# The row of q scores: spread over all partitions by two DMAs instead of eight TensorE transposes

## The chip, the cores and the metric

The kernel runs on one core of a Trainium2 chip, in one launch. The metric is device time in microseconds (us). Five engines work side by side, each through its own list of instructions in order: TensorE (PE in the profile; its weight loads are PEld), VectorE (DVE), ScalarE (ACT), GpSimd (POOL) and SyncE (SP, which here only issues DMAs). Between two instructions of different engines, and between a DMA and its reader, stands a semaphore wait.

## The reference

Two layers on x of 32 batches, each batch C x N = 512 x 1024 in float32; adj is 512 x 512. Cut to what matters:

```python
# layer 0, per batch
q = einsum('c,cn->n', wq, x)                  # 1024 scores
k = einsum('c,cn->n', wk, x)                  # 1024 scores
scores = q[None, :] + k[:, None]              # [m, n]
scores = where(scores > 0, scores, 0.01 * scores)
att = softmax(scores, axis=-1)
agg = einsum('cn,mn->cm', x, att)
x = layernorm(x + relu(adj @ agg + bm))
# layer 1
x = layernorm(x + einsum("nf,nm->mf", x, adj * adj) + bias)
```

In layer 1 `W = adj * adj` elementwise (support and kernel are both adj), and `out[m] = sum_n x[n] W[n, m] + bias`.

## The kernel before

The softmax over a sum q + k with one kink needs no 1024 x 1024 matrix. For each column m the scores above zero are those whose q is over -k, so the kernel sorts: it finds each q's rank, scatters the rows of (adj x)^T to DRAM in the order of q, forms running sums upwards and downwards along the sorted rows, writes both as a table to DRAM, and gathers for every m the one row of the table at which its k falls. Two running sums, weighted and divided, are the softmax-weighted mix.

One batch passes through these steps (short names as they stand in the order lists):

- `ld` loads x (four DMAs of 512 KB, SP). `pa` (PE) computes q and k of the batch in four column groups of 256 (rows 0, 32, 64 and 96 of a PSUM tile hold q, the rows after them k). `pc` (ACT) copies that to SBUF as `part`, 128 x 256. `co` (PE) turns `part` and `cc` (DVE) picks from it `s.qk`: q and k as columns, one element per partition and tile.
- `ro` and `rc` make the **row**: q along the free dimension, the same 1024 values on every partition. `ro` (line 247) is eight TensorE transposes of a column of `s.qk` broadcast to 128 x 128, into a 4 KB PSUM tile; `rc` (line 256) is one DVE instruction that copies the PSUM tile to SBUF as `qb` and takes its maximum on the way (line 261), and two small ones. `qb` has one buffer.
- `rk` (DVE, line 267, eight per batch) compares `qb` with a column of q and counts: ranks. `ct` (ACT, line 281, eight per batch) does it with k by a Sign activation. Both write a `junk` tile that nobody reads.
- `z` (PE, eight of 1/8 batch) is adj x; `zc` (ACT) copies it to `zt`, which has one buffer; `sc` (POOL) scatters it by rank. `sl` loads the sorted rows, `se` (ACT) makes the exponentials, `u` and `d` (DVE) the running sums inside a partition, `cu`, `cd` (PE) and `uc`, `dc` (ACT) the carries over partitions, `tu`, `td`, `te` (DVE) add them, `tw`, `tl` (SP) write the table.
- `g` (POOL) gathers, `mw`, `ms`, `mx` mix, `t` (PE) turns the mix back, `r` (DVE) adds the residual, `s0`, `rt`, `rce`, `n0` (ACT, DVE) are the first layernorm.
- Layer 1 is one level of a Strassen-Winograd product: `t1` to `t4` (DVE) form the sums of quarters of x, `U 11 Z V Y 12 21` (PE) are the seven products (with the bias added by a small bf16 matmul whose stationary operand is `first_0` or `first_10`, 6 x 128), `Uc Vc Zc up lr ll ls` collect them, `s1 r1 n` normalize and `st` stores (four DMAs of 512 KB per batch, SP).

Nothing but order decides when an instruction is issued. `emit` walks three lists of words such as `ro.-1` or `rk.-1.7` (step, batch relative to the iteration, part): `head`, then `loop` once for each of b = 12 to 25, then `tail`. Each word appends its instructions to its engine's list, so the order of words that share an engine is that engine's order. In one iteration of `loop`, layer 1 of batch b-4, the mix of b-3, the table of b-2, the ranks of b-1 and the scores of b are under way. In the list before, `ro.-1` stands near the start of the iteration, followed by `rc.-1` and the ranks; the last part of a batch's `z` (`z.-2.7`) falls into the next iteration:

```
    td.-3.1 ro.-1 tw.-3.0 n0.-4.3 z.-2.7 n0.-4.0 tw.-3.1 tl.-3 t1.-4 rc.-1 U.-4.0 rk.-1.7 U.-4.1
```

A tile of a pool with a tag takes the next buffer of that tag, and its first writer waits until everything that used the buffer before is done. The tags touched here are `qb` (1 buffer), `part`, `carry`, `T2` and `junk_s` (1 each), and `w`: two PSUM tiles of 4 KB, shared by the q row, the four turns and the two `pair` products of a batch.

Of the kernel before, what the change touches and what calls it, by code (L numbers as in the profile page):

```python
# [42 lines left out]
P = 128  # L43
# [6 lines left out]
def adj_resnorm_kernel(  # L50
# [48 lines left out]
    nbm = const.tile([P, CT], F32, name="nbm")  # L99
# [21 lines left out]
    eps = const.tile([P, 1], F32, name="eps")  # L121
    nc.vector.memset(eps, EPS)
    power = const.tile([P, CT], F32, name="power")
# [12 lines left out]
    zero = one.tile([P, ZR], F32, tag="carry", name="zero")[0:1, :]  # L136
    nc.vector.memset(zero, 0.0)
    sorted_z = [dr.tile([N, ZR], F32, name=f"sorted_z_{i}") for i in range(2)]
# [3 lines left out]
    spare = const.tile([1, 1], F32, name="spare")  # L142
# [7 lines left out]
    first_0 = const.tile([6, P], BF16, name="first_0")  # L150
    first_10 = const.tile([6, P], BF16, name="first_10")
# [25 lines left out]
    def bias_parts(b):  # L177


        own = const.tile([6, 8], F32, name="own")  # L180
# [4 lines left out]
        nc.vector.tensor_copy(first_0, own[:, 4:5].broadcast_to([6, P]))  # L185
        nc.vector.memset(first_10, 1.0)
        rest, done = room[:, 0, :], room[:, 1, :]
        for i in range(3):
            part = one.tile([P, N], BF16, tag="junk_s", name=f"bias_part_{i}")[0:6, 0:H]
            nc.vector.tensor_copy(part, rest)  # L190
            if i < 2:
                nc.vector.tensor_tensor(rest, rest, part, ALU.subtract)
            if i == 0:
                nc.vector.tensor_scalar(done, part, own[:, 0:1], None, ALU.mult)
            else:
                nc.vector.scalar_tensor_tensor(
                    done, part, own[:, i : i + 1], done, ALU.mult, ALU.add
                )
# [27 lines left out]
    def parts_copy(b):  # L226
        s = st[b]
        s.part = one.tile([P, Q], F32, tag="part", name=f"part_{b}")
        nc.scalar.copy(s.part, s.ps)
# [8 lines left out]
    def cols_copy(b):  # L238
        s = st[b]
        s.qk = s4.tile([P, NT, 2], F32, tag="qk", name=f"qkc_{b}")  # L240
# [5 lines left out]

    def row(b):

        s = st[b]
        s.ps = p2.tile([P, N], F32, tag="w", name=f"q_tp_{b}")  # L250
        for j in range(NT):
            nc.tensor.transpose(
                s.ps[:, j * P : (j + 1) * P], s.qk[:, j, 0:1].broadcast_to([P, P]), ident
            )

    def row_copy(b):
        s = st[b]
        s.qb = one.tile([P, N], F32, tag="qb", name=f"qb_{b}")
        top = s4.tile([P, 3], F32, tag="top", name=f"top_{b}")
        s.top, s.ntop = top[:, 0:1], top[:, 1:3]  # L260
        nc.vector.tensor_scalar(s.qb, s.ps, 1.0, None, ALU.mult, ALU.max, accum_out=s.top)  # L261
# [19 lines left out]
    def count(b, j):  # L281
        s = st[b]
        junk = one.tile([P, N], BF16, tag="junk_s", name=f"junk_s_{b}_{j}")
        nc.scalar.activation(  # L284
            junk, s.qb, AF.Sign, bias=s.k[:, j : j + 1], accum_out=s.sign[:, j : j + 1]
        )
# [111 lines left out]
    def carry_down_copy(b):  # L398
        st[b].carry = one.tile([P, ZR], F32, tag="carry", name=f"carry_{b}")
# [62 lines left out]
    def stats(b, name):  # L462
        return [sp.tile([P, CT], F32, tag=t + name, name=f"{t}{name}_{b}") for t in ("tot", "var")]

    def spread(b, i, t, v, name):

        junk = one.tile([P, N], BF16, tag="junk_s", name=f"junk_{name}_{b}_{i}")
# [30 lines left out]
    def root0(b):  # L498
            v = st[b].v0
            nc.scalar.activation(v[1], v[1], AF.Sqrt, scale=1.0 / N**3, bias=eps)  # L500

    def root0_end(b):
            v = st[b].v0
            nc.vector.reciprocal(v[1], v[1])  # L504
    
# [39 lines left out]
    def rows1(b, m):  # L545
        s = st[b]
        if not s.v1:
            s.v1 = stats(b, "1")
            s.nb = sp.tile([P, CT], F32, tag="nb", name=f"nb_{b}")
            s.part2 = sp.tile([P, CT], F32, tag="part2", name=f"part2_{b}")  # L550
# [84 lines left out]
    def store(b, m):  # L635
# [7 lines left out]
        "rc": row_copy, "rk": rank, "re": rank_end, "ct": count, "ce": count_end,  # L643
# [21 lines left out]
    bias.0 ld.1 ld.2 ld.3 pa.0 z.0.0 pc.0 co.0 zc.0.0 z.0.1 cc.0 ro.0 zc.0.1 pa.1 rc.0 ct.0.1  # L665
    rk.0.1 z.0.2 ct.0.3 rk.0.7 pc.1 rk.0.2 ct.0.5 z.0.4 rk.0.3 ct.0.2 rk.0.4 ct.0.7 rk.0.6 z.0.6
    zc.0.4 zc.0.2 rk.0.0 rk.0.5 co.1 zc.0.6 z.0.5 re.0 cc.1 ct.0.4 oq.0 sc.0.1 sc.0.6 z.0.3
    sc.0.0 zc.0.5 ct.0.6 sc.0.5 sc.0.2 z.0.7 zc.0.3 sc.0.4 ct.0.0 sc.0.3 ro.1 zc.0.7 sc.0.7
    z.1.0 rc.1 rk.1.3 ct.1.6 ct.1.5 rk.1.1 z.1.6 sl.0.0 sl.0.1 rk.1.7 rk.1.5 z.1.2 zc.1.6 rk.1.6
    ct.1.4 rk.1.0 zc.1.0 se.0.0 oq.1 rk.1.2 z.1.4 se.0.1 u.0.0 ct.1.1 ce.0 u.0.1 u.0.2 z.1.1  # L670
    rk.1.4 u.0.3 u.0.4 z.1.5 u.0.5 zc.1.1 zc.1.4 u.0.6 ct.1.3 u.0.7 zc.1.2 ct.1.7 d.0.7 pa.3
    d.0.6 zc.1.5 re.1 d.0.5 sc.1.1 cu.0 pc.3 d.0.4 ct.1.2 sc.1.5 co.3 z.1.3 d.0.3 uc.0 sc.1.2
    cc.3 d.0.2 ct.1.0 tu.0.0 sc.1.0 sc.1.4 z.1.7 d.0.1 zc.1.3 te.0 sc.1.3 d.0.0 tl.0 tu.0.1
    sc.1.6 cd.0 ro.3 dc.0 zc.1.7 pa.2 td.0.0 sc.1.7 z.2.5 rc.3 tw.0.0 rk.3.0 ct.3.0 ct.3.6
    td.0.1 z.2.0 zc.2.5 ct.3.3 ce.1 tw.0.1 rk.3.6 pc.2 ct.3.1 co.2 z.2.4 rk.3.3 ct.3.2 rk.3.1
    ct.3.4 rk.3.4 ct.3.5 z.2.3 cc.2 rk.3.7 zc.2.0 ct.3.7 rk.3.5 g.0.0 sl.1.0 zc.2.4 sl.1.1 ro.2
    rk.3.2 g.0.3 z.2.6 rc.2 g.0.1 ct.2.4 rk.2.2 zc.2.3 z.2.7 rk.2.6 ct.2.0 rk.2.1 we.0 se.1.0
    ct.2.3 rk.2.5 z.2.1 g.0.2 u.1.0 ce.3 g.0.4 u.1.1 oq.2 u.1.2 g.0.6 se.1.1 zc.2.6 rk.2.0 z.2.2
    zc.2.7 g.0.5 ct.2.7 rk.2.3 g.0.7 mw.0.0 rk.2.4 z.3.0 ms.0.2 ms.0.1 mx.0.2 ms.0.0 rk.2.7
    zc.2.1 ms.0.3 ct.2.1 u.1.3 z.3.4 re.2 mx.0.0 sc.2.6 ct.2.2 mw.0.1 sc.2.5 mx.0.1 ms.0.6  # L680
    mx.0.3 we.1 ms.0.5 z.3.1 sc.2.7 mx.0.6 ms.0.7 mx.0.5 ms.0.4 sc.2.4 mx.0.7 zc.2.2 mx.0.4
    sc.2.0 u.1.4 t.0.3 u.1.5 sc.2.3 t.0.1 r.0.3 sc.2.2 zc.3.4 r.0.1 s0.0.3 t.0.2 sc.2.1 u.1.6
    s0.0.1 t.0.0 r.0.2 z.3.2 u.1.7 s0.0.2 r.0.0 zc.3.0 zc.3.1 d.1.7 s0.0.0 cu.1 d.1.6 z.3.3 oq.3
    zc.3.2 d.1.5 uc.1 d.1.4 rt.0 d.1.3 re.3 d.1.2 z.3.5 zc.3.3 rce.0 d.1.1 n0.0.1 sc.3.3 d.1.0
    n0.0.0 sc.3.1 tu.1.0 n0.0.3 cd.1 sc.3.2 t1.0 U.0.0 dc.1 sc.3.0 zc.3.5 td.1.0 n0.0.2 sc.3.5
    U.0.1 ct.2.6 tu.1.1 tw.1.0 Uc.0.0 11.0.0 ct.2.5 td.1.1 11.0.1 Z.0.0 t2.0 tw.1.1 ce.2 V.0.0
    t3.0 Zc.0.0 we.3 t4.0 12.0.0 Uc.0.1 te.1 Vc.0.0 V.0.1 up.0.0 Z.0.1 Vc.0.1 s1.0.0 sl.2.0 tl.1
    Y.0.1 Zc.0.1 sl.2.1 12.0.1 lr.0.1 Y.0.0 up.0.1 se.2.0 g.1.0 u.2.0 21.0.1 lr.0.0 g.1.3 u.2.1
    21.0.0 se.2.1 g.1.1 u.2.2 ll.0.1 s1.0.1 g.1.2 u.2.3 z.3.6 ld.4 u.2.4 ll.0.0 r1.0.1 u.2.5
    ls.0.0 u.2.6 ls.0.1 u.2.7 r1.0.0 s1.0.3 cu.2 d.2.7 zc.3.6 d.2.6 z.3.7 uc.2 mw.1.0 g.1.7  # L690
    d.2.5 ms.1.0 tu.2.0 ms.1.2 g.1.5 n.0.1 g.1.6 pa.4 d.2.4 s1.0.2 tu.2.1 g.1.4 ms.1.3 z.4.5
    n.0.0 sc.3.6 mx.1.0 zc.3.7 r1.0.3 ms.1.1 d.2.3 pc.4 mx.1.2 d.2.2 co.4 z.4.4 mw.1.1 sc.3.4
    d.2.1 ms.1.7 r1.0.2 mx.1.1 ms.1.4 cc.4 ms.1.6 d.2.0 ms.1.5 ro.4 mx.1.4 zc.4.5 mx.1.6 cd.2
    sc.3.7 n.0.2 mx.1.5 z.4.0 mx.1.7 dc.2 st.0.2 rc.4 st.0.0 st.0.1 mx.1.3 ct.4.1 td.2.0 t.1.3
    zc.4.4 ct.4.6 t.1.1 r.1.3 tw.2.0 n.0.3 z.4.1 td.2.1 ct.4.4 zc.4.0 ct.4.5 r.1.1 tw.2.1 t.1.2
    st.0.3 ct.4.2 te.2 t.1.0 rk.4.6 s0.1.1 z.4.2 r.1.2 s0.1.3 r.1.0 s0.1.2 z.4.3 rk.4.4 s0.1.0
    rk.4.0 rt.1 rk.4.1 sl.3.0 tl.2 z.4.7 zc.4.3 sl.3.1 rce.1 rk.4.2 n0.1.1 rk.4.3 zc.4.1 n0.1.0
    rk.4.7 z.4.6 zc.4.2 se.3.0 g.2.0 rk.4.5 g.2.1 t1.1 n0.1.3 U.1.1 g.2.3 u.3.0 n0.1.2 u.3.1
    g.2.2 11.1.1 u.3.2 Uc.1.1 se.3.1 g.2.5 oq.4 u.3.3 we.2 ct.4.3 11.1.0 re.4 g.2.6 u.3.4 zc.4.7
    t2.1 ct.4.0 g.2.4 Z.1.0 u.3.5 ct.4.7 g.2.7 u.3.6 U.1.0 Zc.1.0 sc.4.3 u.3.7 mw.2.0 sc.4.5  # L700
    Z.1.1 d.3.7 ms.2.2 ce.4 sc.4.0 ms.2.1 d.3.6 ms.2.3 12.1.0 mx.2.2 sc.4.1 Zc.1.1 d.3.5 Uc.1.0
    mw.2.1 V.1.0 sc.4.2 d.3.4 ms.2.7 mx.2.1 zc.4.6 V.1.1 Vc.1.0 mx.2.7 up.1.0 12.1.1 Vc.1.1 t3.1
    s1.1.0 up.1.1 Y.1.0 ms.2.5 r1.1.0 ms.2.4 t4.1 ms.2.6 Y.1.1 ms.2.0 lr.1.0 s1.1.1 mx.2.4
    21.1.0 lr.1.1 r1.1.1 mx.2.0 21.1.1 d.3.3 mx.2.6 mx.2.5 cu.3 sc.4.6 ll.1.1 ld.5 d.3.2 n.1.0
    mx.2.3 d.3.1 ll.1.0 t.2.3 uc.3 ls.1.1 ls.1.0 d.3.0 t.2.2 s1.1.2 r.2.3 cd.3 r1.1.2 r.2.2
    t.2.0 dc.3 s1.1.3 tu.3.0 t.2.1 sc.4.7 n.1.2 r.2.0 pa.5 sc.4.4 s0.2.3 st.1.2 td.3.0 st.1.0
    r1.1.3 pc.5 s0.2.2 co.5 r.2.1 z.5.0 tw.3.0 cc.5 s0.2.1 td.3.1 s0.2.0 ro.5 tu.3.1 rt.2 z.5.2
    n.1.1 rc.5 tw.3.1 n.1.3 st.1.1 rce.2 te.3 z.5.1 n0.2.2 rk.5.6 tl.3 st.1.3 n0.2.3 rk.5.5
    n0.2.0 rk.5.3 11.2.0 ct.5.1 rk.5.7 n0.2.1 11.2.1 sl.4.0 rk.5.4 sl.4.1 ct.5.3 U.2.1 g.3.0
# [253 lines left out]
```

## Time and profile before

| | |
|---|---|
| time, median of 3 runs | 2064.76 us (2064.7 to 2069.11) |
| the profiled execution | 2065.32 us, span 2063.6 us, mean granted clock 0.991 |
| PE busy | 2004.7 us, 97% of the span |
| DVE / ACT / POOL busy | 1674.9 (81%) / 1496.3 (73%) / 874.6 (42%) us |
| DMA | 541.04 MB, mean 262 GB/s |

The span is the time from the first to the last instruction of the profiled execution; its own time has 1.7 us around it. Busy time of PE is from the start of a matmul to its modelled end, and matmuls overlap, so the mean duration of one matmul (593 ns for 128x512) is longer than the distance from one to the next; the distance is what a matmul costs in a full stream, and it is read from a timeline or the chain, not from a mean. A line number in the profile is one of the file before the change.

### The profile page before, as it was taken

The page shows a single profiled execution, that of the slowest core. Times are in us where ns is not written, and L with a number is a line of the kernel's source. Part 1 is how long each engine was busy: PE and PEld are TensorE (multiplying, and loading weights), DVE is VectorE, ACT ScalarE, POOL GpSimd, SP SyncE. Part 2 cuts the span into 40 slices and gives each one's busy share as a digit, 9 for nine tenths or more (in the row PEclk, how much of TensorE's full clock was granted, in tenths as well). Part 3 has the DMA queues.
Part 4 walks back from the last instruction along what each step waited for, and adds up shares of the span by engine and source line. Part 5 has one row for each costly group of instructions (what it writes and reads, how often), then busy time and mean ns, then how long its engine had stood idle before and what let it go on. Part 6 is the DMA issues. An engine that isn't in the chain of part 4 may idle for free. (4 is left out here: it accounts for less than half of the span.)

```text
span 2063.6 us, 22066 instructions
## 1 busy us (share of the span) xinstructions
PE 2004.7 (97%) x6609; PEld 956.7 (46%) x6609; DVE 1674.9 (81%) x2778; ACT 1496.3 (73%) x2560; POOL 874.6 (42%) x1106
## 2 busy tenths in 40 slices
PE   8999999999999999999999999999999999999976
PEld 4444444444444444444444544444444444444432
DVE  6888898798877889887889888789778888789672
ACT  3566787678776777777777777777777777767566
POOL 4344543344343444443444443453444443443421
PEclk9999999999999999999999999999999999999988
DMA  5558776866667766667766767766677766677752
GB/s 226 212 222 312 275 287 266 306 264 257 271 245 291 307 255 246 271 266 292 306 241 250 273 268 296 290 249 258 255 276 306 276 244 268 245 269 273 286 204 82
DMA packets 137967, 541.04 MB, mean 262 GB/s; under 512 B 14404, under 2 KB 14416, under 8 KB 129656
## 3 DMA queue, kind: packets, MB, share of 16 engines
q1 hardware_dynamic: 80464, 337.47, 41.2%
q0 software_dynamic: 57344, 202.15, 26.0%
q8 instruction: 52, 0.85, 0.2%
q14 instruction: 67, 0.55, 0.1%
q10 hardware_dynamic: 40, 0.02, 0.0%
HBM read 270.29 MB, written 269.29 MB: 261 GB/s over the span
## 5 line engine op out<-in xcount | busy, mean ns | idle before, releaser
L310 PE MATMUL z_ps<-adj_t,x 128*128 128x512 f32 x2048 | 906.6, 593 | 0.4 <-ACT zt L316 0.4
L310 PEld LDWEIGHTS z_ps<-adj_t,x 128*128 128x128 f32 x2048 | 384.1, 190 | 448.0 <-issue 439.5
L324 POOL DMA_INDIRECT sorted_z<-zt,to x256 | 377.2, 1473 | 481.0 <-ACT zt L316 403.7
L432 POOL DMA_INDIRECT got<-table,of x256 | 262.2, 1024 | 209.6 <-issue 87.8
L271 DVE SCALAR_TENSOR_TENSOR junk_v<-qb,qkc,tie 128x1024 uint8<-128x1024 f32 x256 | 328.2, 1282 | 4.0
L284 ACT ACTIVATE junk_s<-qb,qkc 128x1024 bf16<-128x1024 f32 x256 | 293.9, 1148 | 18.9 <-DVE qb L261 17.0
L475 POOL TENSOR_SCALAR var<-var 128x1 f32<-128x1 f32 x128 | 46.3, 362 | 461.9 <-ACT junk L468 458.6
L454 ACT ACTIVATE got<-got,w 128x512 f32<-128x512 f32 x256 | 172.2, 713 | 64.2 <-DVE w L449 56.6
L316 ACT COPY zt<-z_ps 128x512 f32<-128x512 f32 x256 | 144.4, 577 | 68.4 <-PE z_ps L310 63.2
L459 DVE SCALAR_TENSOR_TENSOR got<-got,w 128x512 f32<-128x512 f32 x256 | 180.9, 745 | 10.9 <-ACT got L454 10.7
L490 DVE SCALAR_TENSOR_TENSOR x<-agg_ps,nbm,x 128x1024 f32<-128x1024 f32 x128 | 161.4, 1280 | 23.1 <-PE agg_ps L482 22.7
L372 DVE SCALAR_TENSOR_TENSOR tab<-tab,ac 128x513 f32<-128x513 f32 x224 | 168.0, 750 | 3.0
L631 ACT ACTIVATE g<-g,nb,var 128x1024 f32<-128x1024 f32 x128 | 157.8, 1238 | 11.8 <-POOL nb L625 11.8
L468 ACT ACTIVATE junk<-g,tot 128x1024 bf16<-128x1024 f32 x128 | 146.6, 1146 | 21.3 <-DVE g L595 16.8
L362 DVE SCALAR_TENSOR_TENSOR tab<-tab,ac 128x514 f32<-128x514 f32 x192 | 144.5, 752 | 16.9 <-ACT ac L348 11.7
L468 ACT ACTIVATE junk<-x,tot 128x1024 bf16<-128x1024 f32 x128 | 146.8, 1147 | 13.6 <-DVE x L490 8.3
L405 DVE TENSOR_TENSOR tab<-tab,carry 128x2052 f32<-128x2052 f32 x64 | 144.8, 2292 | 11.5 <-ACT carry L387 11.5
L540 PE MATMUL sum_ps<-x,adj 128*128 128x512 f32 x256 | 131.4, 637 | 16.3 <-ACT x L508 16.3
L482 PE MATMUL agg_ps<-ident,got 128*128 128x128 f32 x1024 | 133.4, 278 | 11.2 <-issue 4.7
L508 ACT ACTIVATE x<-x,var 128x1024 f32<-128x1024 f32 x128 | 138.5, 1149 | 0.7 <-DVE var L504 0.6
L601 DVE SCALAR_TENSOR_TENSOR g<-sum_ps,g 128x512 f32<-128x512 f32 x64 | 44.0, 687 | 111.8 <-ACT junk_s L284 75.3
L482 PEld LDWEIGHTS agg_ps<-ident,got 128*128 128x128 f32 x1024 | 115.2, 143 | 36.3 <-DVE x L490 12.2
(121 smaller groups left out, 2698.8 us busy)
## 6 DMA issues: line engine op xcount, KB each, us to landing
table<-tab SPq DMA_DIRECT2D x64, 2056.0 KB
tab<-sorted_z SPq DMA_DIRECT2D x64, 1028.0 KB
x<-in_x_dram SPq DMA_DIRECT2D x128, 512.0 KB
out_dram<-g SPq DMA_DIRECT2D x128, 512.0 KB
sorted_z<-zt,to POOLq DMA_INDIRECT x256
got<-table,of POOLq DMA_INDIRECT x256
adj_in<-in_adj_dram SPq DMA_DIRECT2D x1, 1024.0 KB
table<-end SPq DMA_DIRECT2D x32, 2.0 KB
```

The lines of the kernel that those rows point to most:

```text
L271: nc.vector.scalar_tensor_tensor(junk, s.qb, s.q[:, j : j + 1], tie[:, at : at + N], ALU.subtract, ALU.is_gt, accum_out=s.rank[:, j : j + 1],)
L284: nc.scalar.activation(junk, s.qb, AF.Sign, bias=s.k[:, j : j + 1], accum_out=s.sign[:, j : j + 1])
L310: nc.tensor.matmul(s.z[j], xt[:, c, j * P : (j + 1) * P], adj_t[:, c, :], start=(c == 0), stop=(c == CT - 1),)
L324: nc.gpsimd.indirect_dma_start(out=sorted_z[b % 2][:, :], out_offset=bass.IndirectOffsetOnAxis(ap=s.to[:, j : j + 1], axis=0), in_=zt[:, j ...
L372: nc.vector.scalar_tensor_tensor(v, v, c, s.zs[:, j + 1, 0:D], ALU.mult, ALU.add)
L432: nc.gpsimd.indirect_dma_start(out=s.got[:, j, :], out_offset=None, in_=table[b % 2][:, :], in_offset=bass.IndirectOffsetOnAxis(ap=s.of[:, ...
L454: nc.scalar.activation(down, down, AF.Copy, scale=s.w[:, 1, j : j + 1])
L459: nc.vector.scalar_tensor_tensor(up, up, s.w[:, 0, j : j + 1], down, ALU.mult, ALU.add)
L468: nc.scalar.activation(junk, t, AF.Square, bias=v[0][:, i : i + 1], scale=-float(N), accum_out=v[1][:, i : i + 1],)
L482: nc.tensor.transpose(s.agg[o][:, j * P : (j + 1) * P], s.got[:, j, o * P : (o + 1) * P], ident)
L490: nc.vector.scalar_tensor_tensor(t[:, o, :], s.agg[o], nbm[:, o : o + 1], t[:, o, :], ALU.max, ALU.add, accum_out=s.v0[0][:, o : o + 1],)
L631: nc.scalar.activation(g, g, AF.Identity, bias=s.nb[:, m : m + 1], scale=s.v1[1][:, m : m + 1])
```

## The change

The row of q is no longer made by TensorE. `part`, which `pc` has just written, holds q in four partitions as rows of 256. `qw` (new, SP) stores these four rows, 1 KB each, to a DRAM row of 1024 (two such rows, by batch parity), and `ro` is now a DMA on SP that loads that one row into all 128 partitions of `qb`, 512 KB. `rc` no longer copies: it is a plain maximum over `qb` in SBUF, and the two small instructions after it are as before. `qb` now has two buffers. In the order list `qw` stands shortly after `pc`, `ro` several steps later, and `rc` at the end of the iteration.

To make room for the second `qb`, small tiles are put together: `part` and the carry of the downward sums now use the buffer of `T2`, the zero row that of `end`, several constants share one tile, the two `stats` tiles are one, the junk tiles of ACT are uint8 instead of bf16, and the stationary operand of the bias matmul is one bf16 column broadcast to 128 with step 0 instead of a 6 x 128 tile. The lists `head`, `loop` and `tail` are new throughout; the bias preparation moves behind the first batch's ranks, and the loads of batches 2 and 3 behind the first q rows.

```diff
     def parts_copy(b):
         s = st[b]
-        s.part = one.tile([P, Q], F32, tag="part", name=f"part_{b}")
+        s.part = one.tile([P, 2, H], F32, tag="T2", name=f"part_{b}")[:, 0, 0:Q]
         nc.scalar.copy(s.part, s.ps)
...
+    def row_out(b):
+        rows = q_row[b % 2].rearrange("(g o c) -> g o c", g=CT, o=1)
+        nc.sync.dma_start(
+            out=rows, in_=st[b].part.rearrange("(g r) c -> g r c", g=CT)[:, 0:1, :]
+        )
+
     def row(b):
         s = st[b]
-        s.ps = p2.tile([P, N], F32, tag="w", name=f"q_tp_{b}")
-        for j in range(NT):
-            nc.tensor.transpose(
-                s.ps[:, j * P : (j + 1) * P], s.qk[:, j, 0:1].broadcast_to([P, P]), ident
-            )
-
-    def row_copy(b):
-        s = st[b]
-        s.qb = one.tile([P, N], F32, tag="qb", name=f"qb_{b}")
+        s.qb = sp.tile([P, N], F32, tag="qb", name=f"qb_{b}")
+        nc.sync.dma_start(out=s.qb, in_=q_row[b % 2].partition_broadcast(P))
+
+    def row_max(b):
+        s = st[b]
         top = s4.tile([P, 3], F32, tag="top", name=f"top_{b}")
         s.top, s.ntop = top[:, 0:1], top[:, 1:3]
-        nc.vector.tensor_scalar(s.qb, s.ps, 1.0, None, ALU.mult, ALU.max, accum_out=s.top)
+        nc.vector.tensor_reduce(s.top, s.qb, axis=AX.X, op=ALU.max)
         nc.vector.tensor_scalar(s.ntop[:, 0:1], s.top, -1.0, None, ALU.mult)
...
-        junk = one.tile([P, N], BF16, tag="junk_s", name=f"junk_s_{b}_{j}")
+        junk = one.tile([P, N], U8, tag="junk_s", name=f"junk_s_{b}_{j}")
...
     def carry_down_copy(b):
-        st[b].carry = one.tile([P, ZR], F32, tag="carry", name=f"carry_{b}")
+        st[b].carry = one.tile([P, 2, H], F32, tag="T2", name=f"carry_{b}").rearrange("p i c -> p (i c)")[:, 0:ZR]
...
-    first_0 = const.tile([6, P], BF16, name="first_0")
-    first_10 = const.tile([6, P], BF16, name="first_10")
+    first = const.tile([6, 16], BF16, name="first")
+    first_0, first_10 = first[:, 0:1].broadcast_to([6, P]), first[:, 1:2].broadcast_to([6, P])
```

The list of one iteration, the parts that matter (each line is one engine's order, other engines' words left out):

```
PE before: ro.-1 z.-2.7 U.-4.0 U.-4.1 11.-4.1 11.-4.0 Z.-4.0 ... t.-3.0 co.0 t.-3.2 z.-1.4 z.-1.5 cd.-2 z.-1.6
PE after:  U.-4.0 U.-4.1 11.-4.0 11.-4.1 Z.-4.1 ... t.-3.0 co.0 t.-3.2 z.-1.4 z.-1.5 cd.-2 z.-1.7 z.-1.6
DVE before: td.-3.1 t1.-4 rc.-1 rk.-1.7 ... td.-2.0
DVE after:  t1.-4 t2.-4 rk.-1.5 ... td.-2.0 td.-2.1 rc.0
ACT before: ... dc.-2 zc.-1.5 n0.-3.1 n0.-3.2 | n0.-4.3 n0.-4.0 Uc.-4.0 ct.-1.3
ACT after:  ... dc.-2 zc.-1.5 n0.-3.2 n0.-3.0 n0.-3.1 | ct.-1.1 n0.-4.3 Uc.-4.1
SP before: tw.-3.0 tw.-3.1 tl.-3 sl.-2.0 sl.-2.1 ld.0 st.-4.1 st.-4.0 st.-4.2 st.-4.3
SP after:  sl.-2.0 sl.-2.1 ld.0 st.-4.0 qw.0 st.-4.1 tl.-2 st.-4.2 st.-4.3 ro.0 tw.-2.0 tw.-2.1
SP head after: ld.1 qw.0 ro.0 qw.1 ro.1 ld.2 sl.0.0 sl.0.1 ld.3 qw.3 ro.3 tw.0.0 ...
```

(`|` marks the start of the next iteration, in which the batch counted as -3 is counted as -4.)

## The prediction

> **What bounds the kernel now.** I read the page's busy times first, then busy time by windows, then the groups of instructions for the lines that the change touches, then the chain, and last the timeline of one iteration on PE, DVE and ACT.
>
> ```profile
> PE 2004.7 (97%) x6609; PEld 956.7 (46%) x6609; DVE 1674.9 (81%) x2778; ACT 1496.3 (73%) x2560; POOL 874.6 (42%) x1106
> ```
>
> PE is the only engine without room, on average. An average hides stages, so the windows follow (span, sum, then busy per engine with its count, granted clock, DMA share, GB/s):
>
> ```profile
> 50.00:100.00 50.00, 49.96 (x190) 23.68 (x189) 44.83 (x73) 27.87 (x56) 15.55 (x19) 1.00 0.51 194
> 683.40:1428.90 745.50, 744.29 (x2473) 356.78 (x2472) 620.72 (x1033) 561.82 (x961) 327.54 (x409) 1.00 0.69 272
> 1950.00:2000.00 50.00, 33.91 (x92) 16.80 (x91) 33.64 (x50) 30.56 (x48) 18.11 (x23) 0.83 0.61 230
> ```
>
> 683.4 to 1428.9 is exactly twelve iterations, from one q row to the twelfth after it: 62.12 us each, of which PE is idle 1.2/12 = 0.1 us. DVE has 10.4 us free per iteration, ACT 15.3, the DMA engines 31%. So the loop is bound by PE's list from end to end, and PE's whole idle time, 2063.6 - 2004.7 = 58.9 us, lies for the most part before 300 and after 1930 us. What leaves PE's list in the loop leaves the time, unless another engine turns late.
>
> The groups of the lines that go (busy, mean of one):
>
> ```profile
> L261 DVE TENSOR_SCALAR_CACHE_REDUCE qb<-q_tp 128x1024 f32<-128x1024 f32 x32 | 39.0, 1219 | 18.4 <-PE z_ps L310 11.0 <-PE q_tp L252 7.3 <-ACT junk_s L284 0.2
> L252 PE MATMUL q_tp<-ident,qkc 128*128 128x128 f32 x256 | 33.3, 273 | 0.5 <-DVE qkc L241 0.5
> L252 PEld LDWEIGHTS q_tp<-ident,qkc 128*128 128x128 f32 x256 | 29.5, 137 | 15.9 <-issue 13.3 <-DVE qkc L241 1.6 <-DVE tab L372 0.2
> ```
>
> 273 ns is the length of one transpose with its drain; eight of them overlap. The PE timeline of an iteration shows what they cost in the stream (start, length):
>
> ```profile
> 1043.87 1.04 PE L482 MATMUL agg_ps<-ident,got 128*128 128x128 f32 x8
> 1044.74 7.03 PE L310 MATMUL z_ps<-adj_t,x 128*128 128x512 f32 x16
> 1051.61 1.03 PE L380 MATMUL carry_ps_False<-tab,behind 128*128 128x257 f32 x4
> 1052.48 3.60 PE L310 MATMUL z_ps<-adj_t,x 128*128 128x512 f32 x8
> 1055.91 1.04 PE L252 MATMUL q_tp<-ident,qkc 128*128 128x128 f32 x8
> 1056.79 3.60 PE L310 MATMUL z_ps<-adj_t,x 128*128 128x512 f32 x8
> 1060.32 0.38 PE L538 MATMUL sum_ps<-bias_p,first 6*128 6x512 bf16 x1
> ```
>
> From the row's start to the next z it is 0.88 us; no line carries an idle mark, so every start is the end of the one before. The chain says the same, 0.87:
>
> ```profile
> 1856.68 3.44 PE z_ps L310 x8
> 1860.12 0.87 PE carry_ps_False L380 x4
> 1860.99 0.87 PE q_tp L252 x8
> ```
>
> **The transposes go.** 32 x 0.87 = 27.8 us, all on the path where PE is full. Weight loads run under matmuls and add nothing.
>
> **DVE's step** keeps its place and nearly its size: one maximum over 128x1024 in SBUF for a copy with maximum from PSUM. No plain maximum of that size is in the trace; one-pass DVE instructions over 128x1024 f32 take 1.22 (this one, and the sums at L519 to L533) to 1.28 us (L271). I take 1.2, from below 1.0 if a pass without a large output is cheaper; with 10.4 us free per iteration either end is worth nothing. The Trainium skill, page "VectorE: DVE Perf Modes", "Rules for kernel authors", speaks against this edit: a `tensor_reduce` on the hot path is the slowest DVE operation and should be restructured. By it the maximum runs at one element per cycle, by that page's 0.96 GHz an estimate of 1.1 to 1.3 us, and the sum would be the same; no row here has the operation at this size.
>
> **Two DMAs come.** `qw` is 4 KB in four rows; the nearest row is the 2 KB store of the table's last row, whose completion event came 1.3 us after issue (996.44 to 997.74). `ro` is 512 KB, 4 KB on each partition, as one store or one quarter of an x load: by completion events the store issued at 1044.71 landed at 1047.35 (2.6 us), the first quarter of x issued at 1022.82, in the middle of the gathers, at 1029.3 (6.5). I take 3 to 6.5 us. What hides it: `ro` follows `st.-4.3`, which was issued at 1051.27, so `ro` goes out near 1051.6 and lands by 1054.6 to 1058.1. Who waits:
>
> ```profile
> 1053.42 4.50 DVE L405 TENSOR_TENSOR tab<-tab,carry 128x2052 f32<-128x2052 f32 x2 [0.36 <-ACT carry L387]
> 1053.75 4.28 ACT L508 ACTIVATE x<-x,var 128x1024 f32<-128x1024 f32 x4
> ```
>
> DVE reaches `rc.0` after these two additions, at 1057.9. ACT reaches `ct.-1.1` after three of the four normalizations, at about 1057. Queued behind `ct.-1.1` on ACT is the fourth, which `11.-4.0` needs: with the row gone PE begins layer 1 at 1060.32 - 0.87 = 59.4 and `11` two U's later (2 x 2.2), at 1063.8; the fourth takes 1.15 and the count before it 1.3, so the row may land as late as 1061.3, 9.7 us after issue, before PE loses anything. On DVE `rc` (1.5) and `t1` (1.2) stand before `Z`, which PE reaches two products (3.4) later still. So in the loop the DMA costs nothing, with 3 us to spare over the slowest row.
>
> SP: `qw.0` waits for `pc.0` (1043.5), and holds `st.-4.1`, `tl.-2`, `st.-4.2` behind it; `st.-4.1` moves from 1033.4 to about 1044, its g tile is wanted again after 1062. `ro` waits for `qw`'s landing (1045) and the second buffer, both long past at 1051. The 16.8 MB are 3% of 541; DMA goes from 69 to about 71%. POOL keeps its order but for `sc.-1.0` before `r1.-4.2`. Cost 0.
>
> **The shared buffers** add waits that are met in time: the carry copy `dc.-2` (1052.8) waits for `co.0` and `qw.0` (1044 and 1045), `pc.0` for `V.-4.1` (20 us earlier), `t2` for `td` on its own engine. The PSUM pair `w` has one user fewer. ACT writing uint8 for bf16: 1148 ns (bf16, L284) against 1149 (f32, L508), so the type is not seen; with 15 us free, 0.
>
> **The bias weights with step 0**, four small matmuls per batch: their loads (90 ns) stand exposed, 1060.32 following z by 0.1. Bounds: 0, since L252's loads have step 0 and take 137 ns where the dense ones of L482 take 141; or the 190 ns of a dense f32 load, 128 x 0.1 = 12.7 us. I take 0, the row with the same step.
>
> **The lists.** Loop: between the last turn and the next U stand four z and one carry, 14.6 us, where four z, carry and row made 15.5; but the two normalizations that U needs are done after three, not four. U had 2.2 us to spare, it has 2.5. I take 0. Tail: the order is the same but for neighbours; 0, with 4 either way. Head: `ro.0` must wait for `qw.0`, and that stands in the ring behind x of batch 1, whose last piece landed at 18.5; + 1.3 + 2.6 to 5.3 puts the row at 22.4 to 25.1, against 22.7 before. `rc.1` (1.5) now stands before the last rank of batch 0, so its scatters and its table are 1.2 to 3.9 us later. PE and the first batch's chain meet at 119.8 almost without slack:
>
> ```profile
> 119.81 1.91 PE L482 MATMUL agg_ps<-ident,got 128*128 128x128 f32 x16
> 122.24 0.98 PE L482 MATMUL agg_ps<-ident,got 128*128 128x128 f32 x7 [0.51 <-DVE x L490]
> ```
>
> So the first four rows' 3.5 us are given back there, and 3.9 more at worst; nothing if the 11.0 us that DVE waited for batch 1's row behind PE (L261 above) come to use. I take 3.5.
>
> **Sum.** Against the profiled execution, 2065.3 (0.6 above the median of 2064.76): 2065.3 - 27.8 + 3.5 = 2041.0.
>
> **Rivals.**
> The row lands too late (slower). If the spreading load is served by few DMA engines, the fill takes long: the x quarters land 1.28 us apart on sixteen engines, so one engine would take 16 x 1.28 = 20.5 us, 10.8 beyond the cover of 9.7. `ct` and the fourth normalization then hold PE in every iteration: 2041 + 32 x 10.8 = 2387. It decides from 9.7 us after issue; four engines (5.1 us) stay inside. No load with a repeated row of this size is in the trace; all 512 KB rows speak for sixteen. On this the Trainium skill, page "DMA: Bandwidth & Descriptors", "Rules for kernel authors", says that a leading step-0 dimension of fewer than 16 copies confines a DMA to as many engines. With 128 copies that rule would leave all sixteen, and the sum stays; no run here shows it. 8 in 100.
>
> The gain drowns (no change): head, exposed bias weights and new small waits at their upper ends, 7.4 + 12.7 + 0.1 x 32 = 23.3, leave 2061. Against it: each alone is unlikely. 4 in 100.
>
> DVE or ACT becomes the bound: they'd need 62.1 us of work per iteration and have 51.7 and 46.8; the time would be PE's again. Not counted. That PE isn't relieved could only be if the transposes stood in idle time, which the timeline excludes; 1 in 100 for some slower order of lists, near 2075.
>
> **Numbers.** The forecast has 87 in 100; the likeliest time is 2041. Low end 2032: no loss in the head (-3.5) and 5 of the idle time in head and tail regained. High end 2054: all of the weights' 12.7. About 0.2% (4.1 us) is what a measurement here can tell from no change. Faster 0.87, same 0.04, slower 0.09.
>
> **What would show it.** L252 gone; PE some 28 us less busy in 256 fewer instructions; 61.25 us per iteration with PE still idle under 0.3; `rc` at about 1.2 us without a DMA wait; ACT's first count without one; bias weight loads still at 90 ns; idle before the first turns of batch 0. A wait of ACT or DVE for the DMA of `qb` in each iteration would prove the first rival; weight loads near 190 ns the second.

## The result and the profile after

The forecast was 2041 us and faster. The kernel after takes 2078.8 us (median of 20 runs, 2063.98 to 2093.99), the kernel before 2064.99 us in the same session (20 runs, 2060.24 to 2069.11): ratio 1.0063, 95% interval 1.0042 to 1.0084. It is slower, and its runs spread over 30 us where those of before spread over 9. The profiled execution of after took 2069.55 us (span 2067.8, granted clock 0.986), one of its better ones.

The busy line of the page, kernel after:

```profile
PE 1987.2 (96%) x6353; PEld 932.5 (45%) x6353; DVE 1672.2 (81%) x2746; ACT 1486.3 (72%) x2560; POOL 830.8 (40%) x1093
```

TensorE lost exactly the 256 transposes and 17.5 us of busy time, where some 28 were forecast; the span grew by 4.2. So work left PE, and more than that came back as idle time. What the transposes were replaced by is not slow in itself. Next are three lines of the groups of instructions by tile (count: duration least/median/most, first and last start): the maximum, the bias weights, and what DVE waited for ahead of the maximum (us, times).

```profile
L262 DVE TENSOR_REDUCE top<-qb x32: 1206/1213/1221, 21.4 to 1873.2; 128x1 f32<-128x1024 f32 x32
L540 PEld LDWEIGHTS <-first x128: 90/91/98, 133.9 to 2040.9; 6*128 6x128 bf16 x128
  DMA qb<-q_row: 6.2, 4
```

The maximum takes the 1.2 us of the forecast, the bias weights their 90 ns with step 0 too, and DVE waits for the row four times in 32 batches, three times in the head (before 320 us) and once at 1808. By completion events, where all of them are recorded, the 512 KB landed 3.3 to 7.3 us after issue.

Busy time by windows (columns as before), for the start, for twelve iterations from one first product `U` to the twelfth after it, and for the end:

```profile
50.00:100.00 50.00, 48.89 (x176) 22.19 (x175) 39.68 (x63) 27.36 (x60) 17.31 (x20) 1.00 0.76 282
634.50:1377.20 742.70, 735.53 (x2377) 346.49 (x2376) 621.62 (x1020) 556.73 (x961) 292.53 (x396) 1.00 0.73 282
1950.00:2000.00 50.00, 34.40 (x91) 16.23 (x90) 37.38 (x57) 30.69 (x49) 19.83 (x23) 0.76 0.60 235
```

Twelve iterations take 742.7 us, 61.9 each, where before took 62.12: 0.2 us less, not 0.87. PE is idle for 0.6 us per iteration, not 0.1. But this is a mean of two kinds. One by one, the iterations of after take 61.03 us, again and again, or anything from 61.1 to 64.1. 61.03 is 0.87 less than the 61.9 of an undisturbed iteration before. The forecast's saving is there in every clean iteration, and lost in the others.

It helps to cut the span at two places: the first `U` of batch 7, where the head's irregular order ends, and that of batch 24. The forecast for the three stretches is that of before less 11, 17 and 4 transposed rows of 0.87, plus the 3.5 for the head.

| | head, to `U.7` | to `U.24` | to the end | span |
|---|---|---|---|---|
| before | 562.8 | 1058.7 | 442.1 | 2063.6 |
| forecast | 556.7 | 1043.9 | 438.6 | 2039.2 |
| after | 573.4 | 1049.8 | 444.6 | 2067.8 |
| after, another execution (e0) | 575.2 | 1065.5 | 443.0 | 2083.7 |

The head alone misses the forecast by 16.7 us, the loop by 5.9 in this execution and by 21.6 in another, the end by 6.0. The other one, e0's profiled execution, is the slowest of its twelve, so the two rows span most of what after does. PE by windows in the head, before and then after (length, PE busy, clock, DMA share, GB/s):

```profile
0.00:562.80 562.80, 545.54 (x1868) 1.00 0.68 262
```

```profile
0.00:573.40 573.40, 542.38 (x1779) 0.98 0.70 266
```

PE is idle for 31.0 us in place of 17.3, and part of its matmuls run at half the clock. After's head has four stretches at a granted clock of 0.50, 20.5 us in all (after, then the only one of before):

```profile
181.88:185.29 3.41, 3.41 (x7) 0.50 0.03 12
284.28:291.11 6.83, 5.33 (x7) 0.50 0.00 0
359.37:362.78 3.41, 3.41 (x33) 0.50 0.02 5
547.10:553.93 6.83, 3.82 (x20) 0.50 0.20 77
```

```profile
180.57:183.98 3.41, 3.41 (x6) 0.50 0.20 77
```

PE is busy for 16.0 us in after's four, so the half clock costs at most 8.0 us there (an estimate, half of the busy time), against 1.7 before. The loop of this execution has no such stretch.

**One stall of the loop, followed back.** The timelines of PE, DVE, ACT, SP and POOL in the iteration that begins at 818.7 (start, length, instruction, and in brackets the idle time before it and what ended it):

```profile
841.25 1.88 PE L542 MATMUL pair_ps<-x,S 128*128 128x512 f32 x4
845.43 1.98 PE L542 MATMUL sum_ps<-zt,adj 128*128 128x512 f32 x4 [2.30 <-DVE g L603]
847.26 9.17 PE L311 MATMUL z_ps<-adj_t,x 128*128 128x512 f32 x21
...
844.28 0.49 DVE L358 TENSOR_SCALAR tab<-tab,ac 128x514 f32<-128x514 f32 x1 [3.43 <-ACT ac L349]
844.69 0.68 DVE L603 SCALAR_TENSOR_TENSOR g<-sum_ps,g 128x512 f32<-128x512 f32 x1
...
843.95 0.30 ACT L349 ACTIVATE ac<-tab,top 128x4 f32<-128x4 f32 x1 [6.78 <-DMA tab<-sorted_z]
...
831.84 0.92 SPq L344 DMA_DIRECT2D tab<-sorted_z  x2
...
826.71 1.51 POOL L325 DMA_INDIRECT sorted_z<-zt,to  x1 [10.85 <-ACT zt L317]
```

Read it from the top. PE's product `21.-4.1` waits 2.3 us for DVE's `lr.-4.1` (L603). DVE wasn't slow: in its list `u.-2.0` (L358) stands ahead of `lr.-4.1` and itself waits 3.4 us for ACT's `se.-2.0` (L349), which waits 6.8 us for the load of the sorted rows of batch b-2. That load goes out when POOL has scattered the last pieces, and POOL, in the new list, first waits for piece 7 (`sc.-2.7`), whose copy comes last, and only then issues the piece that is ready (`sc.-2.6`). In the median of 16 iterations the load is issued 12.9 us after the first `U`, before 11.8. None of the words in this chain is the row's. They belong to the new lists. And where the kernel before had 3.44 us of `z.-1.0` between `12.-4.1` and `21.-4.1`, the new list puts the two products back to back. PE of before at the same place, without an idle mark:

```profile
834.23 1.88 PE L540 MATMUL pair_ps<-x,S 128*128 128x512 f32 x4
835.94 3.60 PE L310 MATMUL z_ps<-adj_t,x 128*128 128x512 f32 x8
839.38 1.88 PE L540 MATMUL sum_ps<-zt,adj 128*128 128x512 f32 x4
```

The load of the sorted rows was just as late in that iteration of before, 13.4 us after its first `U` (825.14 against 811.7), and this product didn't wait.

### The profile page after: what moved, and what is told of

Its sections match the earlier page's. It is cut to its first block, busy times and chain, and to the rows that moved or that the text cites. A ratio compares the mean times of both kernels' runs of the same rounds, so it can differ in the third digit from the quotient of the medians.

```text
span 2067.8 us, 21566 instructions
## 1 busy us (share of the span) xinstructions
PE 1987.2 (96%) x6353; PEld 932.5 (45%) x6353; DVE 1672.2 (81%) x2746; ACT 1486.3 (72%) x2560; POOL 830.8 (40%) x1093
## 5 line engine op out<-in xcount | busy, mean ns | idle before, releaser
L325 POOL DMA_INDIRECT sorted_z<-zt,to x256 | 339.1, 1325 | 618.5 <-ACT zt L317 363.5
L433 POOL DMA_INDIRECT got<-table,of x256 | 270.4, 1056 | 243.8 <-issue 91.2
L285 ACT ACTIVATE junk_s<-qb,qkc 128x1024 uint8<-128x1024 f32 x256 | 294.3, 1150 | 8.8 <-DVE bias_in L195 4.2
L477 POOL TENSOR_SCALAR tv<-tv 128x1 f32<-128x1 f32 x128 | 43.1, 336 | 338.2 <-ACT junk L470 332.1
L492 DVE SCALAR_TENSOR_TENSOR x<-agg_ps,small,x 128x1024 f32<-128x1024 f32 x128 | 161.1, 1277 | 13.5 <-PE agg_ps L484 12.0
L633 ACT ACTIVATE g<-g,nb,tv 128x1024 f32<-128x1024 f32 x128 | 157.7, 1239 | 5.2 <-POOL nb L627 5.1
L470 ACT ACTIVATE junk<-x,tv 128x1024 uint8<-128x1024 f32 x128 | 146.7, 1146 | 20.3 <-DVE x L492 13.6
L470 ACT ACTIVATE junk<-g,tv 128x1024 uint8<-128x1024 f32 x128 | 147.0, 1149 | 19.1 <-DVE g L597 15.5
L603 DVE SCALAR_TENSOR_TENSOR g<-sum_ps,g 128x512 f32<-128x512 f32 x64 | 44.0, 688 | 130.9 <-PE sum_ps L542 122.3
L510 ACT ACTIVATE x<-x,tv 128x1024 f32<-128x1024 f32 x128 | 140.0, 1149 | 3.8 <-DVE tv L506 3.8
```

The source lines that it names most:

```text
L285: nc.scalar.activation(junk, s.qb, AF.Sign, bias=s.k[:, j : j + 1], accum_out=s.sign[:, j : j + 1])
L325: nc.gpsimd.indirect_dma_start(out=sorted_z[b % 2][:, :], out_offset=bass.IndirectOffsetOnAxis(ap=s.to[:, j : j + 1], axis=0), in_=zt[:, j ...
L433: nc.gpsimd.indirect_dma_start(out=s.got[:, j, :], out_offset=None, in_=table[b % 2][:, :], in_offset=bass.IndirectOffsetOnAxis(ap=s.of[:, ...
L470: nc.scalar.activation(junk, t, AF.Square, bias=v[0][:, i : i + 1], scale=-float(N), accum_out=v[1][:, i : i + 1],)
```

## The experiments

The theories named in the expectations: **L**, that the two DMAs are as cheap as forecast where they are issued early enough, and that the loss is a matter of places in the lists. **D**, that the DMAs as such disturb other work, by their traffic or by SP's waits. Each kernel is compared with the kernel before in runs on the same chip. The experiments were made on four chips, on which the median of before is 2063.79 to 2067.12 us; where two experiments of different chips are compared, the difference of each from its own before is taken. The stretches (head, loop, end) are those of the one profiled execution of each kernel. The kernels on the old lists have the shared buffers of the change, but `part` has a buffer of its own. All of these make at least the first four rows by transposes.

**e1, the old lists.** Order lists of before; `qw` behind `pc`, `ro` at the place where the transposes stood:

```diff
-    ... pc.0 ...            ro.-1 z.-2.7 ... rc.-1
+    ... pc.0 qw.0 ...       ro.-1 z.-2.7 ... rc.-1     (ro is now the load, on SP)
```

> The three order lists of before, with the row of q by two DMAs from batch 4 on (the store right after the copy of the scores, the load where the transposes stood), the first four rows still by TensorE. Theory L (the new lists lose what the DMAs gain): 28 rows x 0.87 = 24.4 us come off, 2065 - 24 = 2041, iterations of 61.2 us. Theory D (the DMAs themselves disturb: their traffic and SP's waits make the sorted rows late): iterations stay at 61.8 to 62, time 2058 to 2075, and the spread of runs is as wide as in the changed kernel (30 us).

Measured: 2069.6 us against 2067.12, ratio 1.001 (0.9998 to 1.0022). The time lies in the range of D, and the iterations are those of L: in the loop they take 61.03 to 61.1 us for the most part, so the loop of after does lose by its list. But the place of the load is bad: six of the 28 rows come late, four of them in the head. The worst, on SP and on DVE:

```profile
1675.56 2.53 SPq L438 DMA_DIRECT2D table<-tab  x2
1678.14 1.14 SPq L441 DMA_DIRECT2D table<-end  x1
1679.38 0.95 SPq L268 DMA_DIRECT2D qb<-q_row  x1
```

```profile
1689.80 1.22 DVE L277 TENSOR_REDUCE top<-qb 128x1 f32<-128x1024 f32 x1 [12.07 <-DMA qb<-q_row]
```

The row's load stands in SP's queue behind the table of 2 x 2056 KB, and DVE waits 12.1 us for it. That iteration took 70.46 us. Nine such waits of DVE and ACT sum to 41.6 us; where both wait for one row, it counts twice.

**e2, the new lists alone.** The kernel after with the row made by TensorE as before, at the place of `ro` or, where `cc` comes later, right behind it:

```diff
-        nc.sync.dma_start(out=s.qb, in_=q_row[b % 2].partition_broadcast(P))
+        (eight transposes into PSUM; rc copies with maximum, as before)
```

> The changed kernel with its new lists and shared buffers, but the row of q by TensorE's eight transposes again (at the place of the load, in the first batches as soon as the columns are there), without the two DMAs. Theory L: the new lists are slow by themselves, so the transposes come on top of the changed kernel's 2079: about 2085 to 2105. Theory D: without the DMAs the new lists are as good as the old ones, 2060 to 2070.

Measured: 2087.09 us against 2067.12, ratio 1.0088 (1.0074 to 1.0102): 20.0 us slower, without a row DMA in it. What PE waited for from `U.7` on (us, times, longest; L624 of this file is after's L603):

```profile
PE sum_ps L563 <- DVE g L624: 15.0, 7, 2.8
PE agg_ps L505 <- DVE x L513: 2.6, 7, 0.4
```

The stall of the loop is the same one, with transposes. Its profiled execution is the slowest of its five, 27.6 us over that of before: 18.2 of them lie in the loop (1076.9 against 1058.7), 9.0 in the head (571.8 against 562.8), 0.4 at the end.

**e0, after once more, and e3, one exchange.** In e3 two words of the loop list of after change places, so that POOL issues the ready piece first:

```diff
-    ... sc.-2.7 rk.-1.7 ct.-1.2 sc.-2.6 ...
+    ... sc.-2.6 rk.-1.7 ct.-1.2 sc.-2.7 ...
```

> The changed kernel as it is, on the same chip as the three others, for a reference: 2064 to 2094 as in its twenty runs, median 2079.

> The changed kernel with one swap in the loop's list: the scatter of part 6 of a batch ahead of that of part 7, in the order in which ScalarE copies them. In the changed kernel the load of the sorted rows is issued 12.9 us after the first U of an iteration, before at 11.8. If that delay is what stalls TensorE later in the iteration (theory L, second half of it), the load goes out at about 11.8 to 12.2 again, the waits of ScalarE for the sorted rows fall, and 14 iterations win 0.3 to 0.6 us each: 4 to 9 us less than the changed kernel. Theory D: no difference over 2 us.

Measured: e0 2075.64 us, ratio 1.0034 (1.0017 to 1.0052); e3 2066.75 us, ratio 1.0003 (0.9987 to 1.0018). One exchange of two words takes 9 us off, at the upper end of what L expected (4 to 9). The load of the sorted rows goes out at 11.6 us instead of 13.0. The loop of e3's profiled execution, one of its better ones, takes 1042.5 us; after's took 1049.8 in one of its better ones and 1065.5 in e0's slowest.

e0 also shows what a small stall can cost. PE's timeline and PE by windows (granted clock the third last column) around its stall at 852:

```profile
847.67 1.88 PE L542 MATMUL pair_ps<-x,S 128*128 128x512 f32 x4
852.31 2.95 PE L542 MATMUL sum_ps<-zt,adj 128*128 128x512 f32 x4 [2.77 <-DVE g L603]
```

```profile
848.00:852.00 4.00, 1.55 (x4) 1.00 1.03 411
852.00:856.00 4.00, 3.69 (x6) 0.65 1.03 406
```

The product behind a pause of 2.77 us takes 2.95 us instead of 1.88, at a granted clock of 0.65, and the iteration 66.02 instead of 61.03: 5.0 us for a stall of 2.8. Behind the 2.30 us stall shown above the clock stayed at 1.00. But the length of the pause doesn't decide it. In the same execution PE waited longer for the same sum, at 660.7, and the next product took its usual time:

```profile
663.86 1.98 PE L542 MATMUL sum_ps<-zt,adj 128*128 128x512 f32 x4 [3.16 <-DVE g L603]
```

```profile
664.20:668.00 3.80, 3.80 (x10) 1.00 1.03 406
```

That iteration took 64.45 us, 3.4 for a pause of 3.16. Of the five stalls of 1.5 us and more in e0's loop those of 2.77 and 2.55 us were followed by 3.41 us at half the clock and cost 5.0 and 4.6 us; those of 3.16, 3.10 and 1.50 us were not. The two stretches of low clock:

```profile
853.19:856.60 3.41, 3.41 (x5) 0.50 1.04 403
1163.80:1167.21 3.41, 3.05 (x4) 0.50 1.04 409
```

In e2 a stall of 2.27 us lowered the clock and one of 2.71 didn't. What decides it, the runs don't show. The Trainium skill, page "TensorE: Matmul & The Clock Gate", Part 1, gives the rule as no idle gaps of PE over some 3.4 us. By it none of these pauses would have cost any clock. Here three of them did.

**e5, the exchange and the cover.** e3, and `21.-4.1` behind `z.-1.0` again:

```diff
-    ... 12.-4.1 ... mw.-3.0 21.-4.1 ... z.-1.0 ld.0 ...
+    ... 12.-4.1 ... mw.-3.0         ... z.-1.0 21.-4.1 ld.0 ...
```

> The changed kernel with two edits in the loop's list: the scatter swap, and the product 21 of the second half behind the first z instead of directly behind product 12 (as in the old list), so that 3.44 us of other work of TensorE stand between. Theory L: with the sorted rows in time and the wait of TensorE for VectorE's sum covered, every iteration takes 61.0 us, 0.3 less than with the swap alone: 2 to 5 us under it, and the spread of runs, which comes from that wait, falls from 15 to 20 us to under 8. The head's loss of 11 us stays: about 2060 to 2064. Theory D: no change.

Measured: 2057.68 us against 2063.79, ratio 0.9969 (0.9959 to 0.9979). It is faster than the expected 2060 to 2064, and the spread, 12 us, didn't fall under 8. Against its own before it stands at -6.1 us, where e0 stands at +8.5: two moved words are worth some 15 us, with the row's DMAs untouched.

**e12, the cover alone.** The kernel after with only the second edit of e5.

> The kernel after with one word of its loop list moved: product 21.-4.1 of layer 1 behind the 3.44 us of z.-1.0 again, as the kernel before has it; the exchange of the two scatters, which e5 has too, is left out. Theory L: ACT and DVE still run 3 us later in each turn, but PE has work while they do, so the 2 to 3 us stalls and the low clock behind them are gone: iterations of 61.0 to 61.3, median 2056 to 2062, between e3 (2066.75) and e5 (2057.68) and nearer to e5. If the stall only goes to the next product that waits for the late chain, iterations stay mixed (61 to 65) and the median is 2068 to 2077, like the kernel after.

Measured: 2070.79 us (2067.72 to 2077.24) against 2064.82, ratio 1.0037 (1.0024 to 1.0051). This contradicts the number given for L, and agrees with the other case that the expectation names. It stands at +6.0 against its own before, 2.6 under e0, which isn't clear of the spread of the runs. PE's waits in the loop:

```profile
PE agg_ps L484 <- DVE got L460: 4.9, 14, 0.7
PE agg_ps L484 <- DVE x L492: 4.3, 11, 0.7
```

The wait for L603 is gone, and PE now waits for the next thing that the late chain delays, the mixed rows for the turn `t.-3`. Iterations of 63.7 us remain. The cover hides a late chain for one product only. Of the 15 us that both words give back, the exchange, which brings the load forward, gives 9 alone; the cover gives some 3 alone, and 6 on top of the exchange.

**e6, the old lists with the load early.** e1, with `ro` moved from the transposes' place to right behind `qw`:

```diff
-    ... pc.0 qw.0 ...       ro.-1 z.-2.7
+    ... pc.0 qw.0 ro.0 ...        z.-2.7
```

> The old lists with the DMA row from batch 4 on, as in the first run, but SyncE issues the load right behind the store, ahead of the stores and table writes that stood in its queue before the load. In the first run VectorE and ScalarE waited up to 12 us for the row where the load stood behind table writes. Theory L (now: the row costs nothing where it is issued early enough, and all losses are places in lists): those waits vanish, 28 rows come off in full, iterations 61.05 us, 2065 - 24 to 28 = 2037 to 2043. Theory D (traffic of the DMAs, or SyncE's wait for the store's landing, makes other transfers late): 2055 or more.

Measured: 2052.86 us against 2063.79, ratio 0.9951 (0.9938 to 0.9963). PE by windows from `U.7` to `U.28`:

```profile
573.70:1855.50 1281.80, 1281.80 (x4160) 1.00 0.74 286
```

Twenty-one iterations of 61.04 us in the mean and not a gap in PE: the forecast's loop, 0.2 us per iteration better than the 61.25 that it named. In the loop the DMAs cost nothing. But the head is 573.7 us, 10.9 more than before, with lists that are those of before, and the time falls between the ranges of L and D.

**e7, the traffic twice.** e6 with the 512 KB load issued twice per batch:

```diff
+        for _ in range(2):
             nc.sync.dma_start(out=s.qb, in_=q_row[b % 2].partition_broadcast(P))
```

> As the run before, but SyncE issues the spreading load of 512 KB twice in a row for every batch from 4 on: twice the suspected traffic, 14.7 MB more, same result. Theory L: the second load stays under cover too, within 3 us of the run before. Theory D: the loss by traffic doubles, 10 us or more over it.

Measured: 2076.01 us, ratio 1.0053 (1.0037 to 1.0068), 23.2 more than e6. Of the 26.2 us between the spans, 14.5 fall in the head, 9.0 at the end and 2.7 in the loop. A second 512 KB is almost free where PE's list is deep, and dear where it waits for a chain. So D holds in the head and at the end, and L in the loop. The edit doubles more than the traffic: both loads write the same buffer, and SP issues the second when the first has landed, 3.5 to 4.6 us later, with the table writes behind it (SP's queue for batch 5):

```profile
257.96 0.33 SPq L269 DMA_DIRECT2D qb<-q_row  x1
```

```profile
261.45 0.32 SPq L269 DMA_DIRECT2D qb<-q_row  x1
262.07 0.79 SPq L439 DMA_DIRECT2D table<-tab  x2
```

So e7 doesn't tell traffic from SP's wait.

**e8 and e9, which rows of the head.** e6, with the rows of batches 0 to 7 (e8), or of 0 to 3, 5 and 6 (e9), by transposes:

```diff
     def by_pe(b):
-        return b < 4
+        return b < 8                      # e9: b < 4 or b in (5, 6)
```

> The kernel before's lists; the rows of batches 0 to 7 by TensorE's transposes (in e6 0 to 3), the other 24 by way of DRAM, issued early as in e6. Theory L (a row costs nothing where it is issued early enough; what the head lost belongs to the rows of batches 4 to 7, whose DMAs stand on SP's queue between the table writes of batches 2 to 5, where the cycle table, sums, table has no slack): first U of batch 7 between 559 and 563 us (before 562.8, e6 573.7), iterations of 61.03 from there, 24 x 1.0 less than before: span about 2038, median 2038 to 2043, ratio 0.988. Theory D (the DMAs' traffic as such is what the head can't bear): rows 8 to 11 still lose there, first U of batch 7 at 567 or later, median 2046 or more.

> As e6, but of the head's rows only those of batches 0 to 3, 5 and 6 by TensorE; 4 and 7 to 31 by way of DRAM. Theory L, in its narrow form (two rows make the head's loss: row 5 goes out in front of the table write of batch 3 and holds SP's queue 3.3 us while it waits for its own landing; row 6 stands in the rings behind the table write of batch 4 and comes late): first U of batch 7 between 558 and 564 us, 61.03 after that, median 2036 to 2043, like e8 or up to 2 us below. If rows 4 and 7 cost as much as 5 and 6 (theory D), about half of e6's 10.9 us stays: first U of batch 7 near 568, median near 2047.

Measured: e8 2043.75 us (2042.89 to 2047.38) against 2063.79, ratio 0.9897 (0.9883 to 0.9912), the fastest kernel here: 1.0% faster than before, with 24 of the 32 rows by DMA. e9 2048.94 us (2041.9 to 2050.37), ratio 0.9913 (0.9896 to 0.9931). Four rows of the head fewer by DMA make e8 9.1 us faster than e6, although 3.5 us of transposes come back: 12.6 us for four rows (before has the same median beside both). The narrow form of L falls by the median. Rows 4 and 7 would cost about as much as 5 and 6, for e9 stands near the middle; but its six runs lie in two groups, two at 2042 and four at 2049 to 2050, so this split is weak. e8's own profiled head (566.5) is above its expected 559 to 563, and its median 0.75 above the range; the profiled execution was the slowest of its four.

**e10 and e11, traffic or queue.** Both are e8 plus, for batches 4 to 7, half of what the row's DMAs do in e6:

```diff
+    def row_extra(b):                                        # e10
+        t = sp.tile([P, N], F32, tag="qb", name=f"extra_{b}")
+        nc.sync.dma_start(out=t, in_=x[b, 0, :].partition_broadcast(P))
...
+    def row_extra(b):                                        # e11
+        (the 4 KB store of row_out)
+        nc.sync.dma_start(out=q_end[b % 2], in_=q_row[b % 2])
```

> e8 (rows 0 to 7 by TensorE) and, for batches 4 to 7, one more load where e6 has the row's two DMAs: 512 KB of an input row spread over all partitions into the free row buffer; nothing is computed from it, no store goes ahead of it and it waits for no other DMA. It has the row's traffic without the row's wait. e8: 2043.75 us; e6, whose four rows go by both DMAs and leave out 32 transposes: 2052.86. Reading Q (what the head lost is SP's queue: it waits for the 4 KB store to land while table writes stand behind it): as e8, 2043 to 2046. Reading T (the 512 KB on the rings delay the tables and gathers behind them): 12.6 us more in full (9.1 between e8 and e6, and the 3.5 us of transposes that e6 saves), 2052 to 2058.

> e8 and, for batches 4 to 7, at the same place in SP's queue, the row's 4 KB store and behind it a copy of those 4 KB from DRAM to DRAM, which waits until the store has landed as the spreading load of e6 does; no 512 KB load, and nothing is computed from the copy. It has the row's wait without its traffic. Reading Q: most of the 12.6 us, 2050 to 2057 (a part of e6's loss is a row that comes late, which can't be seen here). Reading T: as e8, 2043 to 2046.

Measured: e10 2051.52 us (2049.55 to 2053.15) and e11 2046.13 us (2043.53 to 2051.09), both against 2064.82. Traffic without the wait costs 7.8 us over e8, the wait without traffic 2.4, of the 12.6; before is 1.0 us slower on this chip than on e8's, so against their own before it is 6.7 and 1.4. Neither reading has it alone, but more than half of it is the traffic. The cost of the wait is no more than such runs spread. The split rests on medians of five runs and four: in the profiled executions the heads of e10 and e11 are equal (570.8 us). The wait itself is in e11's profile. SP's queue (start, length):

```profile
248.93 0.54 SPq L257 DMA_DIRECT2D q_row<-part  x1
252.09 0.53 SPq L260 DMA_DIRECT2D q_end<-q_row  x1
252.93 3.66 SPq L446 DMA_DIRECT2D table<-tab  x2
```

SP stands still for 2.6 us until the 4 KB have landed, and the table of batch 3 goes out behind that, at 252.93 where it went at 251.11 in e8 and at 249.28 before. The rest, 2.4 to 4.5 us by subtraction, would be rows that come late; that these make up the rest isn't shown, but e6 has one, with DVE waiting 3.5 us for the row of batch 6:

```profile
323.93 1.22 DVE L277 TENSOR_REDUCE top<-qb 128x1 f32<-128x1024 f32 x1 [3.53 <-DMA qb<-q_row]
```

## Why the prediction was wrong

The sum 2065.3 - 27.8 + 3.5 had a right first term, a second, the head, that was too small, and a third, the lists, that was taken as nothing. Of the 28.6 us by which the profiled execution misses the forecast span, 16.7 lie in the head, 5.9 in the loop and 6.0 at the end; in e0's, 18.5, 21.6 and 4.4 of 44.5.

- **Transposes, -27.8: right.** Clean iterations are 0.9 to 1.1 us shorter in every kernel with the DMA row (61.03 against 61.9 to 62.1), and e6 runs 21 of them in a row without a gap.
- **DVE's step, uint8, bias weights: right.** 1.21 us, 1.15 us and 91 ns. The rule of the Trainium skill weighed there (page "VectorE: DVE Perf Modes", "Rules for kernel authors"), `tensor_reduce` as the slowest operation, doesn't show: 1213 ns against the 1219 of the copy that it replaced.
- **DMAs in the loop, 0: right for this place.** The row landed 3.3 to 7.3 us after issue, under the 9.7; the longest wait for it in after's loop was 0.5 us. The first rival (few engines, 2387) is refuted by that landing time, and e6 and e7 agree. e1 shows that this belongs to the place: with the load at the transposes' own place, six of 28 rows came late.
- **Lists, loop: the step that failed.** "U had 2.2 us to spare, it has 2.5. I take 0." I compared what stands between the last turn and the next `U`, because the row had stood there, and I didn't follow the rest of a list that I knew to be new throughout. Two of its places decide: POOL's order of two scatters, and a product without its cover. e2 prices the new lists as a whole at 20.0 us (with the shared buffers), most of it in the loop; e3 and e5 give 9 and 15 of it back by one and two moved words.
- **Clock: missing.** The sum has no term for it. In the loop a stall of 2.8 us cost 5.0, because PE came back at half the clock, but only two of e0's five long stalls did that, and none in the profiled execution of after. Between these two loops lie 15.7 us, of which 10.6 are idle time and at most 3.2 (half of PE's busy time at half clock) the clock, so most of the spread is the stalls themselves. The clock weighs more in the head: at most 8.0 us in after against 1.7 before.
- **Lists, tail, "0, with 4 either way": a little too small.** From `U.24` to the end the kernels with the new lists take 442.4 to 445.3 us, those with the old lists and an early row 438.9 to 439.9 (e7 aside): 2 to 7 us.
- **Head, +3.5 (0 to 7.4): too small.** I looked at the first four rows only, and at the first meeting of PE with batch 0's chain. Rows 4 to 7, at 0 in the sum, cost 12.6 us on the old lists (e6 and e8), of which 6.7 to 7.8 is traffic (e10). "The 16.8 MB are 3% of 541" was a mean over the run. That 512 KB among the tables and gathers of the head delay the path to the next product is the likely reading; no delayed transfer was followed to PE. The new head list, with transposes, takes 9.0 us more than before in e2's one profiled execution; with the DMA rows it takes 567.0 (e5) to 575.2 us (e0), so one execution says little to within some 8 us.

Added up on medians: the new lists alone +20.0 (e2), the DMA rows alone on the old lists -10.9 (e6), together +9.1; after was measured at +13.8 and, in e0, at +8.5. This is a rough agreement only: e6 issues the load at another place than after does, and keeps four rows on TensorE. The sign came from the last rival, "some slower order of lists, near 2075", which had 1 in 100.

What stays open: what lowers the clock behind one pause and not behind another, and what of the head's loss is the clock; the first four rows by DMA weren't tried apart from the new lists, and the new head list wasn't taken to pieces. What the shared buffers cost by themselves wasn't measured; e8 has nearly all of them and is 20.0 us faster than before, where its 24 rows at 0.87 make 20.9, so it can't be much.

## What to carry to other kernels

When a change rewrites an order list, price the list and not only the operation: go through it engine by engine, ask of every waiting word what used to stand between it and its releaser, and run the old order with the new operation, and the new order with the old one. Here an added DMA was free only in the stretch where the bound engine has work in stock; in the pipeline's start and end it cost time, so try the old form there (e8: eight rows by TensorE and 24 by DMA, 1.0% faster than before). A stall of TensorE costs its length and, in some cases, up to some 2 us more of lowered clock (e0).

## What was not expected of the hardware

- Pauses of TensorE of 2.27 (e2), 2.55 and 2.77 us (e0) were followed by 3.41 us at half the granted clock, while pauses of 2.30 (after), 2.71 (e2), 3.10 and 3.16 us (e0) were not: the length of the pause doesn't tell.
- A load of one 4 KB DRAM row into 128 partitions, 512 KB written, landed in 3.3 to 7.3 us amid other traffic, about as an ordinary 512 KB load of x amid the gathers of the kernel before (6.5 us).
- A second such load in every batch, with SP's wait for the first, cost 2.7 us over 17 iterations of the loop, 0.16 us each, and 14.5 us in the head, at a DMA share of 0.76 and 292 GB/s in the loop.
